# PSUM of a typed graph network: one standing tile for sums, weights and queries, two banks for node chains, and 806 gather slots in 49 blocks

## The chip, the cores and the metric

The kernel runs on one core of a Trainium2 chip. The time is the device time of one execution in microseconds (us), from the first instruction to the last and what lies around it. The engines are named as the profile names them: PE (matrix products) with its weight loads PEld, DVE (vector engine), ACT (scalar engine), POOL (GpSimd; here it issues the indirect DMAs, that is gathers and scatters of rows), SP (plain DMAs). SBUF is the working memory, PSUM the eight banks into which PE writes and which DVE and ACT read and write.

## The reference

A graph of 6,250 nodes (128 features, 16 node types) and 100,000 edges (32 edge types, sorted by target) goes through two layers of typed attention with 8 heads of 16 features, then a linear layer, a residual and a layer norm. The core of a layer:

```python
k = typed_linear(x, ntype, Wk).reshape(n, H, HS)      # the weight is chosen by the node's type
q = typed_linear(x, ntype, Wq).reshape(n, H, HS)
v = typed_linear(x, ntype, Wv).reshape(n, H, HS)
kT = jnp.einsum('nhd,htdo->nhto', k, Watt)            # for every node and every edge type
vT = jnp.einsum('nhd,htdo->nhto', v, Wmsg)
kw = kT[src, :, etype]
m = vT[src, :, etype]
a = jnp.einsum('ehd,ehd->eh', kw, q[dst]) * pri[:, etype].T / SQRT_D
att = edge_softmax(a, dst, n)                         # over the edges that end in one node
hag = jax.ops.segment_sum((m * att[:, :, None]).reshape(-1, H * HS), dst, num_segments=n)
h = jax.nn.silu(typed_linear(hag, ntype, Wa))
alpha = jax.nn.sigmoid(skip[ntype])[:, None]
h = h * alpha + x * (1.0 - alpha)
return layernorm(h) * g + b
```

All is float32.

## The kernel before

**Tables.** For each layer there is a table in DRAM with one row for each node and edge type: 128 numbers of kT and 128 of vT. An edge is one row of it, and so one row of a gather. Layer 0's table is made in the preparation. Layer 1's is made while layer 0's edges run: `table_block` (L342) multiplies the k and v of 128 nodes by the block-diagonal matrices `bdk` and `bdv` (PE, L354) into PSUM tiles "tb" of two banks, ACT copies each to the SBUF tile "st" (L362; in the last superblock DVE takes some, L360), and an indirect DMA from POOL's queue scatters "st" (L1761). A block of 128 nodes has two such scatters and eight "tb" tiles.

**Blocks and slots.** The preparation sorts the nodes by class (four classes of four node types) and by degree, and puts them into 49 blocks of 128. Each class has 11 blocks of its own, with 25, 21, 19, ... 11 slots (`OWN_SLOTS`, L47). A slot is one edge of each of the 128 nodes, so one gather of 128 rows. What a class's blocks don't hold goes to five mixed blocks of all 16 types (`MIXED_SLOTS`, L48). The first mixed block, `TOP`, has 42 slots, of which it gathers 26 and two more with shared rows, so 28. A layer has 819 gathers. If some block did not hold its nodes' degrees, the kernel would take a slow arm (`arm(False)`, L1916) that handles any graph.

**The edge loop** (`edges`, L1303, once for each layer) goes through the blocks in superblocks of up to four: each class's own, with a mixed superblock behind each of the first two classes. For every four slots (a chunk) it takes one of 12 "kv" tiles, issues four gathers (L1528), multiplies the k half by the block's query q (DVE, L1544) and sums over each head (L1550). When a block's chunks are through, the generator `finished` (L1365) does its softmax and its weighted sum while the next block's chunks run: mask, maximum, difference, exponential on ACT into w, sum "den", products of w and v, sums in "acc" (four slots wide), and the closing sum over these four. A "kv" tile comes free when its v half has been added.

**Node work.** When a superblock is finished, `nodes` (L1626) normalizes, transposes, applies Wa by type, mixes with the old rows, normalizes again, and in layer 0 makes the next k, v and q by type. A typed product is made of masks: for each type, DVE multiplies the node columns by (type == t) into one of four "xm" tiles (`masked`, L287), and PE adds the product with that type's weights to a PSUM tile "nb". Own superblocks have 4 types to go through, mixed ones 16. The queries of the next superblock are made the same way (`queries0`, L1281). All these steps are generators; `spread` and `tick` (L1312, L1316) deal them out among the chunks, so many steps for so many slots. `Held` (L257) keeps node work on DVE, ACT and PE behind the last instruction of the edge stream in program order; POOL's instructions run in program order; for the other engines the compiler's scheduler chooses the order.

**PSUM, eight banks.** In both layers: one bank for "nb" (pool `nps`, L1217), one for `hold`, three two-bank tiles "tb" (pool `tps`, L1220). In layer 0 q is read from SBUF, w lies in `hold`, "acc" in SBUF. In layer 1 each block takes a "tb" tile as `pair` (L1352): q and w in its second bank, "acc" in its first. `moved` (L1356) carries the shared rows of block `TOP` through PE.

Of the kernel before, what the change touches and what calls it, by code (L numbers as in the profile page):

```python
# [20 lines left out]
P = 128  # L21
# [25 lines left out]
OWN_SLOTS = (25, 21, 19, 18, 17, 16, 15, 15, 14, 12, 11)  # L47
MIXED_SLOTS = (42, 20, 16, 14, 9)  # L48
# [24 lines left out]
def kernel(  # L73
# [240 lines left out]
    def linear_of(pool, nps, types, ntb, hT, n, w):  # L314
# [3 lines left out]
        if len(types) > TC:  # L318
            h2 = pool.tile([P, SB * P], F32, name="h2", tag="hb")
            on.scalar.copy(h2[:, :n], hT[:, :n])  # L320
            yield
            hT = h2
# [880 lines left out]
    def arm(fast):  # L1203
# [13 lines left out]
        nps = ctx2.enter_context(tc.tile_pool(name="nps", bufs=1 if fast else 5, space=PSUM))  # L1217

        hold_ps = ctx2.enter_context(tc.tile_pool(name="hold", bufs=1, space=PSUM)) if fast else None
        tps = ctx2.enter_context(tc.tile_pool(name="tps", bufs=3, space=PSUM))  # L1220
# [82 lines left out]
        def edges(l):  # L1303
# [43 lines left out]
            def query(s, i):  # L1347


                if l == 0:  # L1350
                    return got[s][0][:, i, :], None
                pair = tps.tile([P, 2, SB * P], F32, name="tb")  # L1352
                nc.scalar.copy(pair[:, 1, :D], got[s][0][:, i, :])  # L1353
                return pair[:, 1, :D], pair

            def moved(pair, by, what, to):  # L1356


                n = what.shape[1]
                ps = pair[:, 1, D:D + n] if pair is not None else tps.tile(  # L1360
                    [P, 2, SB * P], F32, name="tb")[:, 0, :n]
                nc.tensor.matmul(ps, by, what, start=True, stop=True)
                nc.scalar.copy(to, ps)

            def finished(s, i, chunks, kvt, a, pair, sums, den):  # L1365
# [6 lines left out]
                if i0 + i == TOP:  # L1372
                    rest, chunks = kvt[-1], chunks[:-1]
                    moved(pair, node_of, rest[:, 3, :RK * REST * H],
# [13 lines left out]
                if rest is None:  # L1388
                    if l == 0:
                        held = hold_ps.tile([P, SB * P], F32, name="hold")  # L1390
                    w = (pair[:, 1, D:D + K * H] if l else held[:, :K * H]).rearrange(
                        "p (k h) -> p k h", h=H)
                on.scalar.activation(w, av, AF.Exp)
                if rest is not None:
                    moved(pair, rows_of, a[:, OWN:K, :].rearrange("p k h -> p (k h)"),
# [5 lines left out]
                if rest is None and l:  # L1401
                    acc = pair[:, 0].rearrange("p (k c) -> p k c", k=CH)
                else:
                    acc = ep.tile([P, CH, D], F32, name="acc", bufs=1)
# [23 lines left out]
                if rest is not None:  # L1428
# [14 lines left out]
                    moved(pair, node_of, rest[:, 2, D:], rest[:, 2, :D])  # L1443
# [7 lines left out]
                if i == k - 1:  # L1451
                    spread(work, nodes(l, *sbs[s], sums, den, *got[s][1:], lambda gen: table(s, gen)),
                           (42 if l else 33) + (0 if len(sbs[s][2]) == TC else 14 if l else 58),
# [39 lines left out]
            q, pair = query(0, 0)  # L1493
            for s, (i0, k, types) in enumerate(sbs):
                asked = None
                if s + 1 < len(sbs):
                    asked = queries(got, *sbs[s + 1])
                    spread(work, asked, 25 if mixed(s + 1) else 11 if l == 0 else 8, asking(s))
                sums = ep.tile([P, SB, D], F32, name="sums")
                den = ep.tile([P, SB, H], F32, name="den")  # L1500
                for i in range(k):
# [20 lines left out]
                    for j0, j1 in chunks:  # L1522
# [18 lines left out]
                        if rest:  # L1541
                            moved(pair, rows_of, got[s][0][:, i, :], kv[:, 2, :D])
# [24 lines left out]
                    before = finished(s, i, chunks, kvt, a, pair, sums, den)  # L1567
                    q, pair = then[0] if then else (None, None)
# [57 lines left out]
        def nodes(l, i0, k, types, sums, den, ntb, hr, table):  # L1626
# [46 lines left out]
            if not last:  # L1673
                if fast and i0 == sbs[0][0]:
                    scale_edge_weights()
                if fast and len(types) > TC:
# [6 lines left out]
                    for j in range(3):  # L1683
                        outs.append(nps.tile([P, SB * P], F32, name="nb"))
                        for t0 in range(0, TY, 2):
                            xms = list(masked(npl, types[t0:t0 + 2], ntb, h2, n))
                            yield
                            for t, xm in xms:
                                on.tensor.matmul(outs[j][:, :n], wkqv[:, j, t, :], xm[:, :n],
                                                 start=(t == 0), stop=(t == TY - 1))  # L1690
                            yield
                        if j < 2:
# [270 lines left out]
```

## Time and profile before

| | |
|---|---|
| median of 3 runs | 3025.17 us (3024.95 to 3028.88) |
| the profiled execution, its own time | 3024.62 us |
| its span, first to last instruction | 3022.8 us |
| POOL busy | 2032.2 us (67%) |
| DVE busy | 1891.1 us (63%) |
| PE busy | 1580.5 us (52%) |
| ACT busy | 978.7 us (32%) |
| gathers L1528 | 1638, mean 986 ns |

The span is that of one profiled execution, and 1.8 us of its own time lie around it. Busy is the time in which an engine's instructions ran; what an engine waited for is read from the waits, not from the shares. A gather's time in POOL's row is the time in which POOL makes its descriptors, not the transfer's.

### The profile page before, as it was taken

Reading aid. Unit: us, or ns where it says so; the run is one execution under the profiler, and the core shown is the slowest. Engines: PE = TensorE matmul, PEld = TensorE weight load, DVE = VectorE, ACT = ScalarE, POOL = GpSimd, SP = SyncE. Lnnn points to the kernel's source line nnn. Section 1 sums busy time; section 2 is a strip of 40 time slices with the busy share of each in tenths; the row PEclk is TensorE's granted clock in tenths of the full one; section 3 lists DMA queues with packets and bytes.
Section 4 is the critical chain, followed back from the end, with each engine's and each line's share of the span. In section 5 each row is a group of like instructions: output and inputs, shape, how many; then the busy total and the mean of one; then the engine's idle time right before and its main releaser. Section 6 shows DMA issues by size and latency. Waiting matters only on the chain.

```text
span 3022.8 us, 21562 instructions
## 1 busy us (share of the span) xinstructions
PE 1580.5 (52%) x5325; PEld 703.1 (23%) x5325; DVE 1891.1 (63%) x4383; ACT 978.7 (32%) x1635; POOL 2032.2 (67%) x2116
## 2 busy tenths in 40 slices
PE   5999978413667667777777884021122213221212
PEld 2445434201223322332223332010111001000001
DVE  7467655257657766777666653476576667666665
ACT  3887533200434234434444553011111111111111
POOL 3333665477777777777777762777677777777773
PEclk9999777556777777787777786555555556555555
DMA  7999999943677577867788897333334333333331
GB/s 217 416 418 418 394 392 397 371 107 100 234 275 260 197 248 282 297 225 254 271 303 296 330 354 278 105 110 111 92 103 118 111 111 109 112 109 106 106 100 45
DMA packets 163485, 671.37 MB, mean 222 GB/s; under 512 B 52012, under 2 KB 78926, under 8 KB 138302
## 3 DMA queue, kind: packets, MB, share of 16 engines
q0 software_dynamic: 113152, 635.19, 58.6%
q1 hardware_dynamic: 34218, 27.57, 3.3%
q10 hardware_dynamic: 15976, 7.10, 1.0%
q8 instruction: 46, 0.75, 0.1%
q14 instruction: 93, 0.76, 0.1%
HBM read 245.42 MB, written 425.02 MB: 222 GB/s over the span
## 4 chain that ended last, share of the span: by engine, by line
POOL 24%; issue 17%; DMA 16%; DVE 13%; PE 7%; ACT 3%; ACTq 0%; DVEq 0%; POOLq 0%
POOL kv L1528 21%; DMA kv<-tab,ell 14%; PE nb L267 6%; DVE kv L1544 2%; DVE xm L267 2%; PE tb L354 2%; DVE kv L267 2%; DMA tab<-st,row 2%; DVE a L1550 1%; DVE acc L267 1%; ACT L267 1%; POOL tab L1761 1%; DVE tb L267 1%; DVE hs L267 1%; POOL out_dram L1793 1%
## 5 line engine op out<-in xcount | busy, mean ns | idle before, releaser
L1528 POOL DMA_INDIRECT kv<-tab,ell x1638 | 1615.6, 986 | 542.6 <-issue 437.4
L362 ACT COPY st<-tb 128x512 f32<-128x512 f32 (+1 forms) x984 | 681.6, 777 | 535.4 <-PE tb L354 349.8
L1544 DVE TENSOR_TENSOR kv<-kv,tb 128x512 f32<-128x512 f32 (+3 forms) x223 | 142.7, 640 | 381.1 <-DMA kv<-tab,ell 367.4
L1544 DVE TENSOR_TENSOR kv<-kv,q 128x512 f32<-128x512 f32 (+3 forms) x223 | 142.9, 643 | 324.6 <-DMA kv<-tab,ell 316.1
L354 PE MATMUL tb<-bdv,vT 32*128 32x512 f32 x784 | 266.0, 781 | 45.0 <-ACT st L362 41.5
L1550 DVE TENSOR_REDUCE a<-kv 128x32 f32<-128x512 f32 (+3 forms) x446 | 280.8, 632 | 1.3
L354 PE MATMUL tb<-bdv,kvT 32*128 32x512 f32 x784 | 253.7, 790 | 22.9 <-ACT st L362 22.5
L354 PE MATMUL tb<-bdk,kvT 32*128 32x512 f32 x784 | 257.3, 776 | 7.9 <-ACT st L362 7.3
L267 PE MATMUL nb<-xm,wa 128*128 128x384 f32 (+2 forms) x336 | 178.0, 690 | 148.8 <-DVE xm L267 144.2
L267 PE MATMUL nb<-xm,wkqv 128*128 128x384 f32 (+2 forms) x504 | 218.6, 583 | 48.0 <-DVE xm L267 37.0
L1168 POOL DMA_INDIRECT tab<-st,rows x98 | 101.8, 1039 | 197.7 <-ACT st L362 169.4
L360 DVE COPY st<-tb 128x512 f32<-128x512 f32 (+1 forms) x192 | 128.7, 707 | 145.3 <-PE tb L354 74.7
L267 PE MATMUL nb<-by,all_rows 49*128 49x512 bf16 (+2 forms) x30 | 13.3, 442 | 381.6 <-DVE by L267 353.5
L354 PE MATMUL tb<-bdk,kT 32*128 32x512 f32 x784 | 210.6, 785 | 1.7 <-issue 1.6
L267 PE MATMUL nb<-ident,hag 128*128 128x128 f32 x98 | 24.6, 385 | 284.1 <-DVE hag L267 276.4
L1761 POOL DMA_INDIRECT tab<-st,row x98 | 106.1, 1083 | 80.4 <-DVE st L360 28.0
L267 PEld LDWEIGHTS nb<-xm,wkqv 128*128 128x128 f32 x504 | 106.4, 223 | 174.8 <-issue 88.6
L267 PEld LDWEIGHTS nb<-xm,wa 128*128 128x128 f32 x336 | 85.9, 272 | 240.6 <-issue 184.3
L267 DVE TENSOR_TENSOR tb<-kv,tb 128x512 f32<-128x512 f32 (+3 forms) x216 | 138.2, 640 | 0.2
L267 PE MATMUL nb<-xm,wq 128*128 128x384 f32 (+2 forms) x168 | 92.0, 708 | 87.2 <-DVE xm L267 87.1
L354 PEld LDWEIGHTS tb<-bdv,vT 32*128 32x128 f32 x784 | 98.8, 226 | 147.7 <-ACT st L362 118.9
L1353 ACT COPY tb<-hq 128x128 f32<-128x128 f32 x49 | 13.0, 267 | 369.4 <-DVE sums L267 268.8
(348 smaller groups left out, 2519.9 us busy)
## 6 DMA issues: line engine op xcount, KB each, us to landing
kv<-tab,ell POOLq DMA_INDIRECT x1638
hq<-hqx SPq DMA_DIRECT2D x7, 768.0 KB, 4.8
hqx<-hs SPq DMA_DIRECT2D x7, 512.0 KB, 3.5
hq<-hqx SPq DMA_DIRECT2D x5, 576.0 KB, 4.9
hqx<-xr SPq DMA_DIRECT2D x10, 256.0 KB, 19.2
hqx<-hs SPq DMA_DIRECT2D x5, 384.0 KB, 3.2
hr<-hqx SPq DMA_DIRECT2D x7, 256.0 KB, 5.6
tab<-st,rows POOLq DMA_INDIRECT x98
```

What stands on the lines that cost most here:

```text
L267: put = issue(*args, **kwargs)
L354: stream[nc.tensor] = nc.tensor.matmul(pt[:, b], yT[s, i * P:(i + 1) * P], bd[s, tt, :], start=True, stop=True)
L360: nc.vector.tensor_copy(to, pt)
L362: stream[nc.scalar] = nc.scalar.copy(to, pt)
L1168: put = nc.gpsimd.indirect_dma_start(out=tabs[0].rearrange("(n t) c -> n (t c)", t=16), out_offset=bass.IndirectOffsetOnAxis(ap=rows1[:, t ...
L1353: nc.scalar.copy(pair[:, 1, :D], got[s][0][:, i, :])
L1528: get = nc.gpsimd.indirect_dma_start(out=kv[:, j - j0, :], out_offset=None, in_=tabs[l][:], in_offset=bass.IndirectOffsetOnAxis(ap=ell[:, ...
L1544: stream[nc.vector] = nc.vector.tensor_tensor(kk, kk, of.unsqueeze(1).to_broadcast([P, c, D]), op=ALU.mult)
L1550: nc.vector.tensor_reduce(to, kk.rearrange("p k (h d) -> p k h d", h=H), axis=AX.X, op=ALU.add)
L1761: put = nc.gpsimd.indirect_dma_start(out=tabs[1].rearrange("(n t) c -> n (t c)", t=16), out_offset=bass.IndirectOffsetOnAxis(ap=row2[:, tg ...
L1793: put = nc.gpsimd.indirect_dma_start(out=out, out_offset=bass.IndirectOffsetOnAxis(ap=node[:, b:b + 1], axis=0), in_=o[:, i, :], in_offset ...
```

## The change

Three things change, in both layers unless it says otherwise.

1. *Slots.* Each class has ten blocks of its own (21 to 11 slots), and nine blocks are mixed, in three superblocks behind the first three classes. The number of blocks stays 49; the slots that are gathered go from 819 to 806.
2. *PSUM.* "nb" gets two banks instead of one, "tb" two tiles instead of three. The other two banks are one tile `held` that stands for the whole run: bank 0 for "acc", bank 1 for w (first half) and for the queries, which take turns in the last two quarters. ACT copies each block's q there, in layer 0 too. `moved` always takes a "tb" tile.
3. *Mixed node work.* `linear_of` no longer copies a transposed "nb" tile to SBUF before the masks, which read PSUM instead. For k, v and q of a mixed superblock, k and v share one round of masks (32 masks instead of 48), which read the SBUF copy as before. The step counts given to `spread` follow.

```diff
-OWN_SLOTS = (25, 21, 19, 18, 17, 16, 15, 15, 14, 12, 11)
-MIXED_SLOTS = (42, 20, 16, 14, 9)
+OWN_SLOTS = (21, 19, 18, 17, 16, 15, 14, 13, 12, 11)
+MIXED_SLOTS = (42, 25, 24, 23, 22, 20, 16, 15, 9)
...
         types = list(types)
-        if len(types) > TC:
-            h2 = pool.tile([P, SB * P], F32, name="h2", tag="hb")
-            on.scalar.copy(h2[:, :n], hT[:, :n])
-            yield
-            hT = h2
         some, ps = 2 if len(types) > TC else TC, None
...
-        nps = ctx2.enter_context(tc.tile_pool(name="nps", bufs=1 if fast else 5, space=PSUM))
-
-        hold_ps = ctx2.enter_context(tc.tile_pool(name="hold", bufs=1, space=PSUM)) if fast else None
-        tps = ctx2.enter_context(tc.tile_pool(name="tps", bufs=3, space=PSUM))
+        nps = ctx2.enter_context(tc.tile_pool(name="nps", bufs=2 if fast else 5, space=PSUM))
+
+        turn, held = [0], None
+        if fast:
+            hold_ps = ctx2.enter_context(tc.tile_pool(name="hold", bufs=1, space=PSUM))
+            held = hold_ps.tile([P, 2, SB * P], F32, name="held")
+            assert max(OWN, *KB[:TOP], *KB[TOP + 1:]) * H <= 2 * D
+        tps = ctx2.enter_context(tc.tile_pool(name="tps", bufs=2 if fast else 3, space=PSUM))
...
             def query(s, i):
-                if l == 0:
-                    return got[s][0][:, i, :], None
-                pair = tps.tile([P, 2, SB * P], F32, name="tb")
-                nc.scalar.copy(pair[:, 1, :D], got[s][0][:, i, :])
-                return pair[:, 1, :D], pair
-
-            def moved(pair, by, what, to):
+                at = (2 + turn[0] % 2) * D
+                turn[0] += 1
+                nc.scalar.copy(held[:, 1, at:at + D], got[s][0][:, i, :])
+                return held[:, 1, at:at + D]
+
+            def moved(by, what, to):
                 n = what.shape[1]
-                ps = pair[:, 1, D:D + n] if pair is not None else tps.tile(
-                    [P, 2, SB * P], F32, name="tb")[:, 0, :n]
+                ps = tps.tile([P, 2, SB * P], F32, name="tb")[:, 0, :n]
                 nc.tensor.matmul(ps, by, what, start=True, stop=True)
                 nc.scalar.copy(to, ps)
...
                 w = av
                 if rest is None:
-                    if l == 0:
-                        held = hold_ps.tile([P, SB * P], F32, name="hold")
-                    w = (pair[:, 1, D:D + K * H] if l else held[:, :K * H]).rearrange(
-                        "p (k h) -> p k h", h=H)
+                    w = held[:, 1, :K * H].rearrange("p (k h) -> p k h", h=H)
                 on.scalar.activation(w, av, AF.Exp)
...
-                if rest is None and l:
-                    acc = pair[:, 0].rearrange("p (k c) -> p k c", k=CH)
-                else:
-                    acc = ep.tile([P, CH, D], F32, name="acc", bufs=1)
+                acc = held[:, 0].rearrange("p (k c) -> p k c", k=CH)
...
-                           (42 if l else 33) + (0 if len(sbs[s][2]) == TC else 14 if l else 58),
+                           (42 if l else 33) + (0 if len(sbs[s][2]) == TC else 13 if l else 41),
...
-                    spread(work, asked, 25 if mixed(s + 1) else 11 if l == 0 else 8, asking(s))
+                    spread(work, asked, 24 if mixed(s + 1) else 11 if l == 0 else 8, asking(s))
...
                     outs = []
-                    for j in range(3):
-                        outs.append(nps.tile([P, SB * P], F32, name="nb"))
+                    for js in ((0, 1), (2,)):
+                        outs += [nps.tile([P, SB * P], F32, name="nb") for _ in js]
                         for t0 in range(0, TY, 2):
                             xms = list(masked(npl, types[t0:t0 + 2], ntb, h2, n))
                             yield
                             for t, xm in xms:
-                                on.tensor.matmul(outs[j][:, :n], wkqv[:, j, t, :], xm[:, :n],
-                                                 start=(t == 0), stop=(t == TY - 1))
+                                for j in js:
+                                    on.tensor.matmul(outs[j][:, :n], wkqv[:, j, t, :], xm[:, :n],
+                                                     start=(t == 0), stop=(t == TY - 1))
                             yield
-                        if j < 2:
+                        for j in js[:2 - js[0]]:
                             to = npl.tile([P, SB * P], F32, name=f"kvT{j}", bufs=2)
                             on.scalar.copy(to[:, :n], outs[j][:, :n])
                             outs[j] = to
```

With the new lists a class's own superblocks are (21, 19, 18), (17, 16, 15), (14, 13, 12, 11), in the last class (13, 12, 11), (16, 15, 14), (18, 17), (21, 19); the mixed ones are (42, 25, 24), (23, 22, 20), (16, 15, 9). Before, they were (18, 17, 16, 15), (15, 14, 12, 11), (25, 21, 19), in the last class (15, 14, 12, 11), (17, 16, 15), (19, 18), (25, 21); the mixed ones (42, 20) and (16, 14, 9).

## Rows read from the trace of the kernel before

**Rows 1.** Stages: us from:to, length, busy us (instructions) of each engine.

```profile
core 0: us, PE busy (x) PEld busy (x) DVE busy (x) ACT busy (x) POOL busy (x), PEclk, DMA share, GB/s
600.00:1778.00 1178.00, 807.39 (x2492) 328.32 (x2492) 780.16 (x1707) 453.99 (x617) 905.02 (x884) 0.74 0.71 248
1778.00:1875.00 97.00, 66.21 (x233) 28.94 (x233) 44.62 (x95) 44.70 (x58) 28.21 (x29) 0.73 0.83 329
1875.00:2977.00 1102.00, 210.75 (x463) 106.29 (x463) 694.10 (x1693) 146.53 (x302) 827.55 (x864) 0.54 0.37 108
```

**Rows 2.** Timeline of POOL, layer 1: start us, us, instruction, idle before.

```profile
2303.78 0.94 POOL L1528 DMA_INDIRECT kv<-tab,ell  x1 [0.30 <-issue]
```

**Rows 3.** POOL's waits, 600 to 1778 us: us in total, times, longest us.

```profile
POOL kv L1528 <- issue: 209.9, 689, 0.3
...
POOL tab L1761 <- ACT st L362: 5.1, 10, 2.1
```

**Rows 4.** POOL's groups, 600 to 1875 us: busy us, mean ns, idle before.

```profile
L1528 POOL DMA_INDIRECT kv<-tab,ell x815 | 828.4, 1016 | 261.7 <-issue 214.2 <-DMA tab<-st,row 13.6 <-DMA kv<-tab,ell 11.2
L1761 POOL DMA_INDIRECT tab<-st,row x98 | 106.1, 1083 | 80.4 <-DVE st L360 28.0 <-issue 25.8 <-ACT st L362 22.4
```

**Rows 5.** POOL's groups, 1875 us to the end.

```profile
L1528 POOL DMA_INDIRECT kv<-tab,ell x819 | 782.1, 955 | 272.4 <-issue 222.1 <-DVE t L267 12.8 <-DMA tab<-st,row 12.2
```

**Rows 6.** Timeline of DVE and POOL at two places of layer 0.

```profile
1055.07 0.69 DVE L1544 TENSOR_TENSOR kv<-kv,q 128x512 f32<-128x512 f32 x1 [1.25 <-DMA kv<-tab,ell]
1055.19 1.39 POOL L1528 DMA_INDIRECT kv<-tab,ell  x1 [0.30 <-issue]
...
1101.40 0.68 DVE L267 TENSOR_TENSOR acc<-kv,acc 128x512 f32<-128x512 f32 x1
1101.62 1.27 POOL L1528 DMA_INDIRECT kv<-tab,ell  x1 [0.30 <-issue]
```

**Rows 7.** DVE's groups by shape, 600 to 1875 us.

```profile
L1544 DVE TENSOR_TENSOR kv<-kv,q 128x512 f32<-128x512 f32 x184 | 126.8, 689 | 298.4 <-DMA kv<-tab,ell 290.0 <-ACT q L267 7.6 <-issue 0.6
...
L267 DVE TENSOR_TENSOR acc<-kv,acc 128x512 f32<-128x512 f32 x135 | 92.2, 683 | 0.0
...
L267 DVE TENSOR_REDUCE sums<-acc 128x128 f32<-128x512 f32 x49 | 51.0, 1041 | 0.1
L267 DVE SCALAR_TENSOR_TENSOR xm<-ntb,h 128x384 f32<-128x384 bf16 x80 | 41.1, 551 | 8.6 <-PE nb L267 4.0 <-ACT h L267 3.8
...
L267 DVE SCALAR_TENSOR_TENSOR xm<-ntb,h 128x256 f32<-128x256 bf16 x80 | 30.1, 414 | 5.6 <-PE nb L267 5.4 <-ACT h L267 0.2
```

**Rows 8.** DVE's groups by shape, 1875 us to the end.

```profile
L1544 DVE TENSOR_TENSOR kv<-kv,tb 128x512 f32<-128x512 f32 x184 | 126.2, 686 | 360.4 <-DMA kv<-tab,ell 346.7 <-issue 13.4
...
L267 DVE TENSOR_REDUCE sums<-tb 128x128 f32<-128x512 f32 x48 | 32.5, 678 | 0.0
```

**Rows 9.** DVE's waits, 600 to 1875 us.

```profile
DVE kv L1544 <- DMA kv<-tab,ell: 316.1, 125, 7.0
...
DVE den L267 <- ACT hold L267: 21.3, 7, 9.5
```

**Rows 10.** ACT's groups by shape, 600 to 1875 us.

```profile
L362 ACT COPY st<-tb 128x1024 f32<-128x1024 f32 x384 | 372.9, 1020 | 329.5 <-PE tb L354 276.8 <-DMA tab<-st,row 43.4 <-issue 7.2
```

**Rows 11.** ACT's groups by shape, 1875 us to the end: the copy of q.

```profile
L1353 ACT COPY tb<-hq 128x128 f32<-128x128 f32 x49 | 13.0, 267 | 369.4 <-DVE sums L267 268.8 <-DVE rd L267 59.5 <-issue 24.5
```

**Rows 12.** PE's groups by shape, 600 to 1875 us: masked matmuls of three-block superblocks.

```profile
L267 PE MATMUL nb<-xm,wkqv 128*128 128x384 f32 x192 | 81.0, 569 | 15.6 <-DVE xm L267 13.6 <-ACT kvT L267 1.5
```

**Rows 13.** Timeline of PE in the turn: the two matmuls of one "tb" tile.

```profile
1844.38 1.12 PE L354 MATMUL tb<-bdk,kvT 32*128 32x512 f32 x2
```

**Rows 14.** POOL's waits, 1778 to 1875 us.

```profile
POOL tab L1761 <- DVE st L360: 28.0, 2, 26.5
```

**Rows 15.** Line 354 alone, 600 to 1875 us: PE busy, PEld busy.

```profile
600.00:1875.00 1275.00, 429.90 (x1568) 126.61 (x1568) 0.74 0.72 254
```

**Rows 16.** POOL's waits, 1875 us to the end.

```profile
POOL kv L1528 <- DVE t L267: 12.8, 6, 11.3
```

More of the change, by code (lines that the diff above doesn't have):

```diff
@@ L1347, in query, with finished @@
             def query(s, i):
-                if l == 0:
-                    return got[s][0][:, i, :], None
-                pair = tps.tile([P, 2, SB * P], F32, name="tb")
-                nc.scalar.copy(pair[:, 1, :D], got[s][0][:, i, :])
-                return pair[:, 1, :D], pair
-            def moved(pair, by, what, to):
+                at = (2 + turn[0] % 2) * D
[3 more added lines that the diff above has]
+            def moved(by, what, to):
                 n = what.shape[1]
-                ps = pair[:, 1, D:D + n] if pair is not None else tps.tile(
-                    [P, 2, SB * P], F32, name="tb")[:, 0, :n]
+                ps = tps.tile([P, 2, SB * P], F32, name="tb")[:, 0, :n]
                 nc.tensor.matmul(ps, by, what, start=True, stop=True)
                 nc.scalar.copy(to, ps)
-            def finished(s, i, chunks, kvt, a, pair, sums, den):
+            def finished(s, i, chunks, kvt, a, sums, den):
                 i0, k, _ = sbs[s]
@@ L1373, in finished @@
                     rest, chunks = kvt[-1], chunks[:-1]
-                    moved(pair, node_of, rest[:, 3, :RK * REST * H],
+                    moved(node_of, rest[:, 3, :RK * REST * H],
                           a[:, OWN:K, :].rearrange("p k h -> p (k h)"))
@@ L1388, in finished @@
                 if rest is None:
[L1389 to L1392 removed]
+                    w = held[:, 1, :K * H].rearrange("p (k h) -> p k h", h=H)
                 on.scalar.activation(w, av, AF.Exp)
                 if rest is not None:
[L1395 removed]
+                    moved(rows_of, a[:, OWN:K, :].rearrange("p k h -> p (k h)"),
                           rest[:, 3, :RK * REST * H])
@@ L1442, in finished @@
                                             op=ALU.add)
-                    moved(pair, node_of, rest[:, 2, D:], rest[:, 2, :D])
+                    moved(node_of, rest[:, 2, D:], rest[:, 2, :D])
                     yield
@@ L1492, in edges @@
             before = iter(())
-            q, pair = query(0, 0)
+            q = query(0, 0)
             for s, (i0, k, types) in enumerate(sbs):
@@ L1541, in edges @@
                         if rest:
-                            moved(pair, rows_of, got[s][0][:, i, :], kv[:, 2, :D])
+                            moved(rows_of, got[s][0][:, i, :], kv[:, 2, :D])
                         of = kv[:, 2, :D] if rest else q
@@ L1566, in edges @@
                         step(end=True)
-                    before = finished(s, i, chunks, kvt, a, pair, sums, den)
-                    q, pair = then[0] if then else (None, None)
+                    before = finished(s, i, chunks, kvt, a, sums, den)
+                    q = then[0] if then else None
             for _ in before:
```

## The prediction

> **What bounds the kernel now.** I read the table of stages first [rows 1]. It splits the span: preparation to about 600 us, layer 0's edges to 1778, the turn to layer 1 (97 us), layer 1's edges (1102 us), and a tail of 46 us. In both edge stages POOL is the fullest engine. The busy share hides that it is in truth full: after each gather POOL sits idle for 0.30 us that wait on nothing [rows 2], and in layer 0 its waits are 209.9 us of that kind, in 689 pieces of at most 0.3 us, and next to nothing else [rows 3]. So an instruction costs POOL its own time plus 0.30 us: layer 0's body 905.0 + 884 x 0.30 = 1170 of 1178 us, layer 1's 827.6 + 864 x 0.30 = 1087 of 1102 [rows 1]. POOL's cadence sets both.
>
> The gathers differ, though: 1.016 us each in layer 0 [rows 4], 0.955 in layer 1 [rows 5]. Why is to be seen in the timeline [rows 6]. A gather that starts at 1055.19, while the DVE product kv*q (two operands in SBUF; start 1055.07, 0.69 us) runs, takes 1.39 us instead of 0.95. Another, beside the sum acc+kv (SBUF and SBUF, 1101.40 to 1102.08), takes 1.27. Both gathers end about 0.82 us after that DVE instruction's end: they stood still until then. In layer 1 the queries and sums lie in PSUM ("tb").
>
> **The change part by part.**
>
> *Fewer slots.* In each layer the gathers fall from 819 to 806 (4 x 156, and 182 in the mixed blocks, since block TOP fetches 28 for its 42). 13 gathers at 0.95 + 0.30 = 1.25 us are 16.3 us in each layer, both on the path: -32.5 us. The slots still hold the graph: I counted the degrees of the reference's inputs by class. 1130 nodes overflow into the mixed blocks' 1152 places, and no block's largest degree is over its slots. So the fast arm runs.
>
> *Standing tile for sums, weights and queries.* In layer 0, q and acc move from SBUF to PSUM; layer 1 had them there. DVE's product takes the same time (689 [rows 7] against 686 ns [rows 8]). The closing sum takes 678 ns from PSUM [rows 8] instead of 1041 from SBUF [rows 7]: 48 x 0.36 = 17 us off DVE, which waited 316 us for gathers [rows 9], so worth nothing by itself. POOL gains: 806 gathers at layer 1's mean would save 806 x 61 ns = 49 us. The DVE instructions with two SBUF operands that can hold a gather up are, in full widths, kv*q 126.8, acc 92.2 and the masks xm from SBUF 41.1 + 30.1: 290 us [rows 7]. The first two go. Of the masks, the rounds for wq and wa of mixed superblocks now read PSUM; 3 x 32 = 96 from SBUF stay, x 0.551 = 53 us. That is 18% of the 290, and 18% of the 49 are 9 us. I take -40 us, with ends 0 (the length has another cause) and -49.
>
> On this the Trainium skill (SBUF — State Buffer, Who interferes with whom) says that a VectorE instruction with two SBUF inputs contends with a GpSimd instruction that reads SBUF, but it also infers that tensor_tensor does not hold up descriptor generation, because that needs the write interface. The gathers of [rows 6] go against that inference; by it the 40 us would not be had and the sum would be 3002 us, which is rival 2.
>
> *Waits that the standing tile adds.* Each of layer 0's 49 blocks gets an ACT copy of q, 267 ns as in layer 1 [rows 11]: 13 us on an ACT that is busy 454 of 1178 us [rows 1]. Queries and softmax weights of all blocks now share a bank. If accesses are ordered by bank, as I assume, the copy of the next q waits for the product kv*q before it, and the product after it waits for the copy; the exponential likewise stands between two products. Queued behind the copy on ACT are the table copies, for which PE's next table matmuls wait, then the node matmuls behind those; behind the product on DVE is everything, and POOL waits when kv tiles stay taken. The nearest row is layer 0's "den" waiting for the exponential: 21.3 us in 7 waits [rows 9]. The upper end is that for both, 43 us; it lies in 316 us of DVE's idle time, and gathers may run ahead by 12 kv tiles (48 gathers). I take 0.
>
> The skill has a rule that speaks against this part (PSUM — Partial Sum Buffer, PSUM bank collisions raise a hardware error): guard PSUM by bank and quadrant, not by address. Without it (order by address) the copy waits for nothing and the sum stands; by it, if half of the 43 us came through to POOL, the sum would be 2984 us, inside the range. No row of before shows which, since there each block of layer 1 had its own tile.
>
> *Two "tb" tiles instead of three.* A tile takes PE about 1.12 us to fill [rows 13] and ACT 1.02 us to empty [rows 10]. With two, PE fills one while ACT empties the other; with some 0.3 us of handovers the pair turns in 2.4 us, 1.2 a tile; ACT alone would need 1.02. In the body a block's 8 tiles have some 20 us: nothing. In the turn, where POOL waits 28.0 us for table copies [rows 14], the last superblock's 16 tiles stand on the path: 16 x 0.2 = 3 us, upper end 8 (ACT and DVE empty in parallel there, so both openings show).
>
> *Two "nb" tiles instead of one.* A chain's matmuls start at the first mask instead of after the last, and k, v and q no longer wait for the copy before: about 1 us a chain (of 4 masks of some 0.35 us, three wait no more), on the path only in the turn (-1, at most -4) and the tail (-1). Turn together: +2, ends -4 and +8. The tail's last block has 19 slots instead of 21, another 0.7 us: tail -2.
>
> *Nine mixed blocks instead of five.* They make three superblocks with all 16 types instead of two. In layer 0 each costs 64 masks (80 before). That matters where this work meets few gathers. After the third one (16, 15, 9) comes (13, 12, 11): 36 slots x 1.25 + 8 table writes x 1.38 [rows 4] = 56 us of POOL. DVE must do 48 masks x 0.551 = 26 us, 36 slots x 0.68 (four instructions of 0.68 us per four slots [rows 7]) = 24.5, and about 10 of small steps: 61. PE has 64 + 4 matmuls at 0.42 (81.0 us for 192 [rows 12]) = 29, and the tables of four blocks at 429.9/49 = 8.8 [rows 15]: 64. Both are 5 to 8 us over. The densest window of before, behind (16, 14, 9), (64 masks, 66 slots, 6 writes) is by the same count DVE 92 to POOL's 91, and POOL waited for nothing. I charge +10; ends 0 (the kv tiles bridge it) and 30 (twice both excesses, late table writes with it). The windows after the other two have 58 slots and some 5 us to spare.
>
> In layer 1 a mixed superblock costs 16 masks; with one more that is 9 us in a DVE busy 694 of 1102 us [rows 1]: nothing. The wait of 11 to 13 us behind block TOP [rows 16] stays: its kv tiles come free no sooner.
>
> **Sum.** The profiled execution took 3024.62 us (span 3022.8, 1.8 around it), half a microsecond under the median of 3025.17. 3024.6 - 32.5 - 40 + 2 - 2 + 10 = 2962 us.
>
> **Rivals.**
> 1. *Layer 0 becomes bound by DVE and PE.* Faster gathers only reach table writes or kv tiles that are not ready. For: PE is busy 807 of 1178 us [rows 1], and its masked matmuls grow by a fifth (per block 20 rounds of 128 columns for an own one, 80 for a mixed one: 1280 to 1520). Against: in that stage POOL waited 5.1 us for ACT [rows 3], DVE 316 us for gathers. If layer 0 keeps a quarter of its 56 us: 3024.6 - 16 - 14 - 2 = 2992.
> 2. *The long gathers have another cause:* the 40 us stay, 3002 us. Against: the gathers' ends follow DVE's ends.
> 3. *Slower: two tb tiles become the clock of layer 0.* If ACT and PE alternate, 1.12 + 0.3 - 1.02 = 0.4 us per tile is open; 392 tiles (384 and 8) make 157 us, paid by POOL at the table writes: 3024.6 - 74 + 157 = 3108. It decides from the point where 47% of these openings reach POOL. For: filling takes longer than emptying. Against: ACT's table copies fill 372.9 us of the stage [rows 10].
> 4. *The slots don't hold the graph* and the slow arm runs: many times as long. The count above speaks against it.
>
> **Chances and range.** Forecast 0.67 (its own range 2943 to 2982), rival 1 0.20, rival 2 0.05, rival 3 0.07, rival 4 0.01. Low end: all 49 of the gathers, a turn 4 shorter, no stall: 3024.6 - 32.5 - 49 - 2 - 4 = 2937, taken as 2940. High end: 30 of the gathers, stall 30, turn +8, tail as it was: 3000; rivals 3 and 4 and most of 2 stay outside. Within 0.2% (6 us) is what a measurement of this kernel can't tell from no change. Faster: forecast, rivals 1 and 2, less 0.03 for a rival 1 that eats all of it: 0.89; same 0.04; slower 0.07 (rival 4 and most of 3).
>
> **What would show it.** 806 gathers in each layer at the same 0.30 us; layer 0's mean gather near 0.967 us, long ones only beside masks from SBUF; layer 1's stage 16 us shorter; "sums" at 0.68 us in layer 0; any POOL wait of layer 0 in the window behind (16, 15, 9). It is wrong if POOL waits for "st" or for kv tiles all over layer 0, if gathers stay at 1.016, or if DVE waits for ACT's q copies by more than 43 us and POOL with it.

## The result, and the profile after

The changed kernel takes 3034.38 us (median of 9 runs, 3025.92 to 3038.66), the kernel before beside it 3026.26 us (9 runs, 3021.51 to 3032.2). The ratio is 1.0025, 95% interval 1.0013 to 1.0037: 8 us slower, where 2962 us, 2.1% faster, were forecast. The profiled execution took 3037.24 us, 12.6 more than that of before; the accounts below are made against these two.

The table of stages, cut at the last gather of layer 0 and the first of layer 1:

```profile
core 0: us, PE busy (x) PEld busy (x) DVE busy (x) ACT busy (x) POOL busy (x), PEclk, DMA share, GB/s
600.00:1811.00 1211.00, 922.59 (x2640) 371.42 (x2641) 806.63 (x1769) 472.77 (x678) 856.03 (x888) 0.72 0.70 242
1811.00:1913.00 102.00, 78.84 (x247) 33.47 (x247) 32.27 (x63) 45.67 (x60) 12.96 (x14) 0.65 0.73 294
1913.00:2988.00 1075.00, 215.45 (x503) 111.53 (x503) 716.64 (x1719) 153.44 (x308) 815.17 (x851) 0.55 0.37 109
```

[rows 1] cuts the kernel before at 1778 us, 23 us ahead of its last gather of layer 0. Up to that gather the kernel before has:

```profile
600.00:1801.00 1201.00, 828.70 (x2550) 338.31 (x2550) 794.08 (x1741) 468.42 (x634) 922.55 (x902) 0.74 0.71 250
```

So layer 0's body is longer although POOL has less to do in it: it is busy 856 of 1211 us, where it was busy 923 of 1201. POOL's groups in the changed kernel's body (the gather is now line 1519, the table write line 1753), and its waits:

```profile
L1519 POOL DMA_INDIRECT kv<-tab,ell x802 | 768.4, 958 | 251.8 <-issue 204.1 <-DVE held L267 11.7 <-DMA kv<-tab,ell 10.4
L1753 POOL DMA_INDIRECT tab<-st,row x86 | 88.6, 1030 | 103.5 <-ACT st L357 78.1 <-issue 16.6 <-ACT ntb L267 3.5
```

```profile
POOL kv L1519 <- issue: 204.1, 670, 0.3
POOL tab L1753 <- ACT st L357: 78.1, 20, 16.2
...
POOL kv L1519 <- DVE held L267: 11.7, 17, 6.8
```

The gathers did become short: 958 ns on average against 1016 [rows 4]. But the cadence, one instruction after the other with 0.3 us between them, is broken. Where POOL waited 5.1 us for ACT's table copies [rows 3], it now waits 78.1 us, in pieces of up to 16.2 us. The timeline of DVE and POOL shows what became of the gathers of [rows 6]; these masks, the sum and the product now have a PSUM operand, and gathers that start beside them take 0.94 us:

```profile
702.96 1.94 DVE L267 SCALAR_TENSOR_TENSOR xm<-ntb,nb 128x384 f32<-128x384 bf16 x4
703.04 0.94 POOL L1519 DMA_INDIRECT kv<-tab,ell  x1 [0.30 <-issue]
...
705.74 0.70 DVE L267 TENSOR_TENSOR held<-kv,held 128x512 f32<-128x512 f32 x1
706.78 0.94 POOL L1519 DMA_INDIRECT kv<-tab,ell  x1 [0.30 <-issue]
707.12 0.69 DVE L1535 TENSOR_TENSOR kv<-kv,held 128x512 f32<-128x512 f32 x1 [0.69 <-DMA kv<-tab,ell]
```

Another stretch, in the second superblock behind the second mixed one, shows what the table writes wait for (timeline of PE, ACT and POOL):

```profile
1329.60 5.32 PE L267 MATMUL nb<-xm,wkqv 128*128 128x384 f32 x16
1334.85 1.14 PE L349 MATMUL tb<-bdv,kvT 32*128 32x512 f32 x8
1335.92 5.43 PE L267 MATMUL nb<-xm,wkqv 128*128 128x384 f32 x16
1336.05 1.93 ACT L357 COPY st<-tb 128x1024 f32<-128x1024 f32 x2 [7.81 <-PE tb L349]
1338.26 1.01 POOL L1753 DMA_INDIRECT tab<-st,row  x1 [11.72 <-ACT st L357]
1339.57 1.35 POOL L1519 DMA_INDIRECT kv<-tab,ell  x1 [0.30 <-issue]
...
1342.35 7.32 PE L267 MATMUL nb<-xm,wkqv 128*128 128x384 f32 x20
...
1349.60 1.14 PE L349 MATMUL tb<-bdv,kvT 32*128 32x512 f32 x8
...
1350.80 1.93 ACT L357 COPY st<-tb 128x1024 f32<-128x1024 f32 x2 [2.50 <-PE tb L349]
1353.00 1.35 POOL L1753 DMA_INDIRECT tab<-st,row  x1 [8.25 <-ACT st L357]
```

POOL stands 11.72 us at one write and 8.25 at the next. It waits for ACT, ACT had waited 7.81 us for PE, and PE was never idle: between two pairs of "tb" tiles (1.14 us of table matmuls) it runs 5 to 7 us of the mixed superblock's masked matmuls.

The loss sits where such stretches are. Between 600 and 1811 us POOL's idle time beyond 0.31 us per instruction adds up to 84.7 us (before: 3.6); 68.5 us of it lie in these three stretches, one behind each mixed superblock:

```profile
core 0: us, PE busy (x) PEld busy (x) DVE busy (x) ACT busy (x) POOL busy (x), PEclk, DMA share, GB/s
1004.00:1067.00 63.00, 51.69 (x196) 22.11 (x196) 45.49 (x98) 32.42 (x46) 41.69 (x43) 0.91 0.70 251
1278.00:1366.00 88.00, 81.59 (x259) 35.30 (x258) 63.34 (x137) 34.07 (x46) 52.39 (x54) 0.83 0.66 238
1541.00:1660.00 119.00, 110.00 (x333) 47.67 (x332) 79.58 (x180) 48.13 (x69) 64.57 (x67) 0.83 0.64 234
```

PE is busy 243 of these 270 us (90%), DVE 188. In the middle of each PE makes k, v and q of the mixed superblock, and there it has no gap at all, 120.7 of 121 us:

```profile
core 0: us, PE busy (x), PEclk, DMA share, GB/s
988.00:1029.00 41.00, 40.84 (x139) 0.96 0.56 207
1321.00:1363.00 42.00, 41.86 (x140) 0.94 0.49 178
1615.00:1653.00 38.00, 38.00 (x126) 0.94 0.39 138
```

By the gathers' count these bursts lie not in the superblock that follows the mixed one (908 to 992, 1238 to 1322, 1542 to 1602 us), but nearly whole in the one after it (992 to 1078, 1322 to 1414, 1602 to 1695). POOL lost 1.0, 0.1 and 7.9 us in the first kind and 14.7, 21.9 and 26.4 us in the second. PE is the bound there.

### The profile page after: what moved, and what is told of

The parts are those of the page before. It is cut to its first block, busy times and chain, and to the rows that moved or that the text cites. A ratio compares the mean times of both kernels' runs of the same rounds, so it can differ in the third digit from the quotient of the medians.

```text
span 3035.3 us, 22161 instructions
## 1 busy us (share of the span) xinstructions
PE 1712.3 (56%) x5523; PEld 752.7 (25%) x5523; DVE 1923.8 (63%) x4429; ACT 1005.2 (33%) x1702; POOL 1953.3 (64%) x2090
## 4 chain that ended last, share of the span: by engine, by line
POOL 19%; issue 16%; DVE 16%; PE 14%; DMA 12%; ACT 4%; DVEq 0%; POOLq 0%; ACTq 0%
POOL kv L1519 17%; DMA kv<-tab,ell 11%; PE nb L267 8%; PE tb L349 5%; DVE kv L1535 3%; DVE kv L267 3%; DVE held L267 3%; DVE a L1541 2%; ACT st L357 2%; DVE xm L267 2%; DVE hs L267 1%; ACT L267 1%; DMA tab<-st,row 1%; POOL tab L1753 1%; POOL out_dram L1785 1%
## 5 line engine op out<-in xcount | busy, mean ns | idle before, releaser
L1519 POOL DMA_INDIRECT kv<-tab,ell x1612 | 1543.7, 958 | 527.3 <-issue 416.1
L1535 DVE TENSOR_TENSOR kv<-kv,held 128x512 f32<-128x512 f32 (+3 forms) x440 | 281.0, 640 | 548.6 <-DMA kv<-tab,ell 466.6
L267 DVE TENSOR_TENSOR held<-kv,held 128x512 f32<-128x512 f32 (+3 forms) x438 | 283.1, 646 | 8.8
L349 PE MATMUL tb<-bdv,vT 32*128 32x512 f32 x784 | 259.0, 781 | 46.6 <-ACT st L357 42.8
L267 PE MATMUL nb<-xm,wkqv 128*128 128x384 f32 (+2 forms) x600 | 245.8, 568 | 10.3 <-DVE xm L267 10.2
L267 PE MATMUL nb<-xm,wa 128*128 128x384 f32 (+2 forms) x400 | 201.6, 666 | 85.0 <-DVE xm L267 80.6
L267 PE MATMUL nb<-by,all_rows 49*128 49x384 bf16 (+2 forms) x32 | 14.7, 458 | 385.6 <-DVE by L267 359.8
L267 DVE TENSOR_TENSOR kv<-kv,held 128x512 f32<-128x512 f32 (+3 forms) x330 | 204.7, 621 | 2.0
L267 DVE SCALAR_TENSOR_TENSOR xm<-ntb,nb 128x384 f32<-128x384 bf16 (+2 forms) x352 | 179.4, 555 | 41.5 <-PE nb L267 39.8
L267 PEld LDWEIGHTS nb<-xm,wkqv 128*128 128x128 f32 x600 | 127.4, 220 | 138.4 <-DVE xm L267 40.7
L267 PEld LDWEIGHTS nb<-xm,wa 128*128 128x128 f32 x400 | 99.4, 261 | 186.6 <-issue 84.7
L267 PE MATMUL nb<-xm,wq 128*128 128x384 f32 (+2 forms) x200 | 116.0, 736 | 51.0 <-DVE xm L267 51.0
L267 PE MATMUL nb<-ident,hs 128*128 128x128 f32 x98 | 33.8, 465 | 178.5 <-DVE hs L267 178.5
## 6 DMA issues: line engine op xcount, KB each, us to landing
hqx<-xr SPq DMA_DIRECT2D x10, 256.0 KB, 14.7
```

Of the source, the lines that this page charges most:

```text
L267: put = issue(*args, **kwargs)
L349: stream[nc.tensor] = nc.tensor.matmul(pt[:, b], yT[s, i * P:(i + 1) * P], bd[s, tt, :], start=True, stop=True)
L1519: get = nc.gpsimd.indirect_dma_start(out=kv[:, j - j0, :], out_offset=None, in_=tabs[l][:], in_offset=bass.IndirectOffsetOnAxis(ap=ell[:, ...
L1535: stream[nc.vector] = nc.vector.tensor_tensor(kk, kk, of.unsqueeze(1).to_broadcast([P, c, D]), op=ALU.mult)
```

## The experiments

Each kernel's profiled execution is cut at four starts of gathers: the first and last of layer 0, the first and last of layer 1. In the table "lost" is POOL's idle time beyond 0.31 us per instruction between the first two, and "long" the time by which its instructions there exceed 0.95 us, summed; "writes" are the table writes after layer 0's last gather. All in us, worked out from the traces; the ratio is to the kernel before, run beside each. Masks or matmuls that a kernel leaves out are missing from its results, so the kernels with four types, without masks and without matmuls only show where the time goes.

| kernel | layer 0 | lost | long | turn | writes | layer 1 | tail | median | ratio, 95% |
|---|---|---|---|---|---|---|---|---|---|
| before | 1209.3 | 3.6 | 70.4 | 73.6 | 9 | 1100.9 | 47.4 | 3026.26 | 1 |
| changed | 1217.3 | 84.7 | 17.7 | 101.5 | 12 | 1074.8 | 47.5 | 3034.38 | 1.0025, 1.0013 to 1.0037 |
| lists alone | 1251.9 | 66.0 | 70.6 | 92.2 | 12 | 1088.8 | 50.4 | 3079.40 | 1.0178, 1.0156 to 1.0200 |
| PSUM alone | 1166.2 | 15.1 | 16.4 | 87.0 | 9 | 1090.3 | 42.9 | 2978.74 | 0.9849, 0.9827 to 0.9870 |
| two "tb" alone | 1221.3 | 11.0 | 75.1 | 82.1 | 9 | 1104.1 | 47.1 | 3048.64 | 1.0075, 1.0049 to 1.0101 |
| changed, four types | 1154.6 | 24.0 | 14.7 | 98.1 | 11 | 1074.4 | 46.8 | 2973.65 | 0.9824, 0.9803 to 0.9846 |
| PSUM alone, four types | 1156.4 | 5.4 | 15.0 | 83.0 | 8 | 1090.1 | 41.8 | 2966.41 | 0.9809, 0.9791 to 0.9826 |
| changed, longer window | 1215.7 | 81.9 | 19.0 | 99.3 | 12 | 1075.1 | 46.5 | 3026.27 | 1.0002, 0.9992 to 1.0012 |
| changed, no masks | 1197.3 | 69.3 | 13.2 | 103.6 | 12 | 1074.4 | 47.0 | 3018.03 | 0.9985, 0.9975 to 0.9996 |
| changed, no matmuls | 1162.0 | 25.9 | 21.2 | 104.2 | 12 | 1074.7 | 46.6 | 2982.28 | 0.9852, 0.9832 to 0.9872 |

**First attempt, on another chip.** Four kernels were run together: before with the new lists; the changed kernel with the old lists; before with two "tb" tiles; and the changed kernel with three "tb" tiles, for which "nb" goes back to one bank and the sums back to SBUF.

> The kernel before with the new lists of slots alone (819 to 806 gathers, nine mixed blocks); PSUM as before. Theory A (the nine mixed blocks' 16-type work fills PE and DVE, tables come late, POOL waits at the table writes behind each mixed superblock): no gain of the gathers' length, 16 us from layer 1, layer 0 longer by some 60 to 80: 3070 to 3090 us. Theory B (two tb tiles slow the tables down): no new wait here, the 32 us of 26 gathers are had: 2993 to 3000. Theory C (the shared bank puts ACT's copies of q and the exponentials between DVE's products): as B, 2993 to 3000.

> The changed kernel with the old lists of slots (819 gathers, five mixed blocks); PSUM as changed. A: layer 0 keeps the shorter gathers (53 us less held up) and few waits: 2970 to 2990 us. B: tables late all over layer 0 and in the turn, 3050 to 3080. C: DVE waits for ACT's copies as much as in the changed kernel (64 us) and tables are late as there, 3040 to 3060.

> The kernel before with two tb tiles instead of three and nothing else (two banks lie idle; layer 1's blocks take turns in two tiles as well). A: 3026 to 3032. B: POOL waits for st all over layer 0 and the turn is some 15 us longer: 3070 to 3110. C: 3026 to 3032.

> The changed kernel with three tb tiles, for which the sums go back to SBUF in layer 0 and 1, nb to one bank and the mixed masks to rounds for one product each; new lists, and q and w still in one standing bank. A: POOL waits behind the mixed superblocks as in the changed kernel, plus some 17 us of gathers held up by the sums in SBUF and more masks: 3045 to 3070. B: the waits are gone: 2980 to 2995. C: DVE still waits for the copies, 3040 to 3060.

On that chip the kernel before itself took 3404.8 us (7 runs, 3392.3 to 3419.96). The ratios were 1.0229 (1.0163 to 1.0295), 1.0220 (1.0172 to 1.0268), 1.0139 (1.0075 to 1.0204) and 1.0217 (1.0166 to 1.0267). Everything is slower, and in both layers POOL lost 164 to 327 us. The timeline of the run with two "tb" tiles shows a kind of wait that neither trace of the first chip has:

```profile
2710.27 0.18 DVE L267 BATCH_NORM_AGGREGATE mv<-bn 128x2 f32<-128x6 f32 x1 [1.22 <-DVE mv L267]
...
2715.17 0.17 DVE L267 TENSOR_SCALAR v<-mv 128x4 f32<-128x4 f32 x1 [4.13 <-remote]
2715.17 0.30 ACT L267 ACTIVATE rs<-mv,eps 128x4 f32<-128x4 f32 x1 [5.73 <-remote]
```

Both instructions need only mv, made by 2710.45, and both start at 2715.17. With such waits between the engines POOL is not full anywhere, so these four runs cannot separate the theories. The first three kernels were run again on another chip, where the kernel before takes 3026 us; the runs below are from there and from a third chip, where it takes 3025. One thing carried over: "long" was 73.7 and 82.8 us with queries and sums in SBUF, 16.8 with both in PSUM, 54.8 in the fourth kernel, with the queries there alone and all masks read from SBUF.

**The two halves, and two "tb" tiles.** One half of the change each, by the lists or by everything else:

```diff
 # lists alone: before, with
+OWN_SLOTS = (21, 19, 18, 17, 16, 15, 14, 13, 12, 11)
+MIXED_SLOTS = (42, 25, 24, 23, 22, 20, 16, 15, 9)
 # PSUM alone: the changed kernel, with
+OWN_SLOTS = (25, 21, 19, 18, 17, 16, 15, 15, 14, 12, 11)
+MIXED_SLOTS = (42, 20, 16, 14, 9)
 # two "tb" alone: before, with
+        tps = ctx2.enter_context(tc.tile_pool(name="tps", bufs=2 if fast else 3, space=PSUM))
```

> The kernel before with the new lists of slots alone (806 slots, nine mixed blocks in three superblocks), all PSUM tiles as before; the edit of the first experiment on another chip, whose cross-engine waits were lengthened there. Theory A (the mixed blocks' work of sixteen types makes the tables late, in the window behind each mixed superblock and in the turn): the 32 fewer gathers are more than eaten, ratio 1.005 to 1.02 on a chip where before takes some 3025 us, with GpSimd waiting some 80 us or more for ScalarE's st copies in layer 0. Theory B (two table tiles in place of three make the tables late): the lists alone gain their slots, ratio 0.985 to 0.992, and GpSimd's wait for st stays near the 5 us of before. Theory C (queries, weights and sums in one standing tile put ScalarE's copies and VectorE's products behind one another): as B.

> The changed kernel with the old lists of slots (819 slots, five mixed blocks): all the moves in PSUM, none in the lists. Theory A: the gathers' hold-ups of some 53 us in layer 0 fall away and the tables keep up, ratio 0.978 to 0.987. Theory B: the tables are late with the old lists too, ratio 1.00 to 1.01, GpSimd waiting 80 us or more for st in layer 0. Theory C: the gathers' gain is given back at VectorE, which waits for ScalarE's copies into the standing tile; ratio 0.995 to 1.005 with the loss in both layers.

> The kernel before with two table tiles in place of three and nothing else (two banks stand empty). Theory A: ratio 0.999 to 1.005. Theory B: ratio 1.01 to 1.03 with GpSimd waiting for st. Theory C: ratio 0.999 to 1.003.

The halves add up: +53 us for the lists, -47 for the PSUM part, +6 together, and the whole measured +8. Both ratios lie where theory A put them; POOL's wait for table copies with the lists alone is 56.7 us, less than A's 80. That wait in layer 0's body, lists alone, PSUM alone and two "tb" tiles alone (gathers' waits of the PSUM kernel beside it):

```profile
POOL tab L1761 <- ACT st L362: 56.7, 16, 12.1
```

```profile
POOL tab L1753 <- ACT st L357: 15.5, 18, 6.7
POOL kv L1519 <- DVE held L267: 4.9, 10, 2.2
```

```profile
POOL tab L1761 <- ACT st L362: 13.7, 13, 3.9
```

Theory B has a smaller share of its own: with two tiles alone the kernel is 23 us slower, 12 of them in layer 0's body (7.4 as "lost", 4.7 as "long") and 8.5 in the turn. That is between what A and B expected. Theory C falls: it expected a ratio of 0.995 or more for the PSUM kernel with a loss in both layers, and the ratio is 0.9849 and layer 1 is 10.6 us shorter. These three runs say that the lists cost; the next tell which part of them.

**Four types in the mixed blocks.** The twelve other types' masks and matmuls are left out:

```diff
-            mixed = [(NC * CB + i0, k, range(TY)) for i0, k in superblocks(MB)]
+            mixed = [(NC * CB + i0, k, range(TC)) for i0, k in superblocks(MB)]
```

> The changed kernel whose mixed blocks are computed with the four node types of the first class alone, where the reference has sixteen: twelve of sixteen masked products of each of their linear maps are left out in both layers, and the mixed superblocks count as ordinary ones in the interleaving. Gathers, tables and PSUM tiles are those of the changed kernel. Theory A: with that work gone the tables are in time and the gathers run through, ratio 0.955 to 0.972, GpSimd's wait for st in layer 0 back under 15 us outside the turn. Theory B: the tables stay late, ratio 0.995 or more. Theory C: ratio 0.985 to 0.995.

> The changed PSUM tiles with the old lists (five mixed blocks), the mixed blocks computed with the four types of the first class alone, where the reference has sixteen. With nine mixed blocks the same omission gave 61 us. Theory A with a threshold (a mixed superblock's work costs nothing until the window behind it is full): five blocks were hidden, so only 5 to 20 us are gained on the same kernel with sixteen types, ratio 0.978 to 0.983. Rival, a price in proportion to the mixed blocks: 5/9 of 61 us, some 34 us, ratio 0.972 to 0.975.

With nine mixed blocks the twelve types cost 61 us (ratio 1.0025 to 0.9824), with five 12 us (0.9849 to 0.9809; by the two intervals 4 to 21). The 61 us are less than theory A's number, whose lowest gain was 92 us: the turn is still 24.5 us longer than before, and "lost" is 24.0 us, where it was 3.6. That the two "tb" tiles are behind the latter is not shown. The ratio for five blocks lies in the range given for the threshold, outside that of a price in proportion. In the nine-block kernel 62.7 us of it come from layer 0's body and 3.4 from the turn: the turn's length is not the types' doing.

**Which engine.** In the changed kernel the masks beyond the first two types are left out and the first two used for all, or the matmuls beyond the fourth type are left out and the masks made:

```diff
 # no masks (linear_of; the same in nodes for k, v and q)
-            xms = list(masked(pool, types[t0:t0 + some], ntb, hT, n))
+            if t0 == 0:
+                made = list(masked(pool, types[:some], ntb, hT, n))
+            xms = [(t, xm) for t, (_, xm) in zip(types[t0:t0 + some], made)]
 # no matmuls (linear_of; the same in nodes)
+                if t - types[0] < TC:
                     on.tensor.matmul(ps[:, :n], w[:, t, :], xm[:, :n],
-                                 start=(t == types[0]), stop=(t == types[-1]))
+                                     start=(t == types[0]), stop=(t == types[0] + TC - 1))
```

> The changed kernel in which the mixed blocks' masked products (xm) are made for the first two types alone and used for all sixteen, so that 14 of 16 masks of each of their linear maps are left out (some 93 us of VectorE in layer 0) and every matmul and every step of the interleaving stays. Theory A1 (TensorE is what the tables wait for): within 15 us of the changed kernel, ratio 0.998 to 1.004. Theory A2 (VectorE's masks hold the tables and products up): 40 to 60 us less than the changed kernel, ratio 0.982 to 0.990. Theory A3 (the number of steps per slot in the interleaving, whatever they contain): as A1.

> The changed kernel in which the mixed blocks' masks are all made and 12 of 16 matmuls of each of their linear maps are left out (some 102 us of TensorE in layer 0); masks and steps stay. Theory A1: 40 to 60 us less than the changed kernel, ratio 0.982 to 0.990. Theory A2: within 15 us of it, ratio 0.998 to 1.004. Theory A3: within 15 us too, as in the run without masks.

Without the matmuls 52 of the 61 us are gone (ratio 1.0025 to 0.9852), though every mask is made; without the masks 12 us (to 0.9985), although DVE has 80 us less to do (726.2 against 806.6 us busy in the body). POOL's wait for table copies, no masks and then no matmuls, and PE's masked matmuls in the latter:

```profile
POOL tab L1757 <- ACT st L359: 60.6, 16, 15.3
```

```profile
POOL tab L1754 <- ACT st L358: 22.7, 17, 7.4
```

```profile
L267 PE MATMUL nb<-xm,wkqv 128*128 128x384 f32 x264 | 121.2, 625 | 10.4 <-DVE xm L267 10.4
```

Theory A1, TensorE, holds. Theory A3 (the number of steps, which both kernels keep) falls with the run without matmuls. One rival within A1 stays untested: the run takes away PE's work and, with it, the bursts that table matmuls wait behind. No run keeps the work and changes its order, so how much of the 52 us a better order would give back is not known.

**A longer window behind the third mixed superblock.** (16, 15, 14) now stands before (13, 12, 11):

```diff
-                    cut = [(i0 + SB, k) for i0, k in
-                           reversed(superblocks_of_slots(OWN_SLOTS[SB:]))]
+                    cut = [(i0 + SB, k) for i0, k in superblocks_of_slots(OWN_SLOTS[SB:])]
```

> The changed kernel with one change of order: behind the third mixed superblock comes (16, 15, 14), 45 slots, and then (13, 12, 11), 36 slots, where it was the other way. If the short window behind the third mixed superblock is what costs (the prediction's reading), the loss of some 32 us there falls by 10 to 20 us, ratio 0.995 to 1.000. Rival: the work only runs on into the next window, which is now the short one, and the sum stays, ratio 1.001 to 1.005.

The ratio is 1.0002 (0.9992 to 1.0012), between the two. In the profiled executions "lost" fell only from 84.7 to 81.9 us. POOL's losses behind the first two mixed superblocks stay: 36.7 us between 1000 and 1450 us in the changed kernel, 40.3 here; behind the third 34.3 us (1550 to 1700) became 30.1 (1550 to 1750). So the reading that the third window carries it is not borne out: all three do. The longer window also stands in the wrong place: the third burst of PE still runs from 1616 to 1660 us, which is now in the superblock of 36 slots (1618 to 1690), where 18.3 of the 30.1 us are lost.

## Why the prediction was wrong

It failed in the step on nine mixed blocks, charged at +10 us and at most 30: the lists alone made POOL lose 62 us more in layer 0 (3.6 to 66.0), and the twelve further types cost 61 us of the changed kernel. Two things in that step are wrong.

The first is the price of a matmul: "PE has 64 + 4 matmuls at 0.42 (81.0 us for 192 [rows 12]) = 29". The 192 are records, not matmuls. Each of these fp32 products stands in the trace as two. For k, v and q at 384 columns the program issues 16 x 3 for a mixed superblock of three blocks and 4 x 3 for one of its own class. Before that is 48 + 4 x 12 = 96, and the row has 192; after it is 3 x 48 + 8 x 12 = 240, and the row has 480:

```profile
L267 PE MATMUL nb<-xm,wkqv 128*128 128x384 f32 x480 | 188.7, 551 | 9.3 <-DVE xm L267 9.2
```

So the price is 0.84 us, not 0.42, and the step's own sum for the window behind (16, 15, 9) becomes 57 + 35 = 92 us of PE to POOL's 56: 36 over, not 8. For the windows of 58 slots the same count gives 57 + 26 = 83 us of PE to 58 x 1.25 + 6 x 1.38 = 81 of POOL, before transposes: about full, not "some 5 us to spare". Before, behind (16, 14, 9), it is 83 to POOL's 91. The Trainium skill (FP8 and Floating Point Precision, TensorE Precision Notes) says that true FP32 takes four passes through the array. By it, at one column a tick, 384 columns are 1536 ticks, an estimate of 0.64 us at 2.4 GHz and 1.28 at 1.2; the row above has 188.7 / 240 = 0.79 us in a stage with a mean granted clock of 0.72, and 16 records at 1335.92, in a burst with a mean of 0.94, take 5.43 us, 0.68 for each matmul, so the trace agrees.

The second is the place: the step puts all the matmuls of a mixed superblock into the superblock behind it. In the trace those for k, v and q, 48 of the 64, come nearly whole in the one after that. The corrected price alone would give the first two windows 2 us of loss each; what they lost behind them was 14.7 and 21.9. In the superblocks in which the bursts lie PE is busy 74.5, 81.5 and 85.3 us, and by the prediction's prices POOL's work is 48 x 1.25 + 7 x 1.38 = 70 us in the first two and 66 in the third. So PE is over in all three, and that the corrected 36 comes near the 34.3 us lost behind the third mixed superblock is in part luck. (The step's DVE sum for the window of before, 92, comes to 90 by its own terms; nothing hangs on it.)

The other terms:

- *Fewer slots, -32.5:* right. Layer 0's body has 16 POOL instructions less (13 gathers, and 3 writes that moved to the turn), layer 1 13 gathers less.
- *The gathers' length, -40 (0 to -49):* right mechanism, undersized and past its own end: "long" fell by 52.7 us with the change and 54.0 with the PSUM part alone; the table writes became shorter too (1030 against 1083 ns [rows 4]), which the term left out. These runs go against rival 2 and against the inference of the Trainium skill that the prediction names beside it (SBUF — State Buffer, Who interferes with whom).
- *The standing tile's waits, 0 (43 on DVE):* bigger on DVE than the upper end, and still nearly free for POOL. DVE's waits in layer 0's body:

```profile
DVE kv L1535 <- DMA kv<-tab,ell: 175.4, 68, 7.1
DVE kv L1535 <- ACT held L1351: 64.1, 29, 6.2
...
DVE den L267 <- ACT held L267: 37.0, 16, 8.8
```

  101 us where 43 was the bound. DVE's wait for gathers went from 316 us [rows 9] to 175; with the old lists, where this arrangement is the same, POOL lost 15.1 us in all. The order that the prediction assumed is not what the trace shows: where ACT's copies of q waited, it was once for the product kv*q (0.8 us), and else for the closing sum of the block before, whose operand lies in the other bank of the tile:

```profile
ACT held L1351 <- DVE sums L267: 84.1, 19, 12.5
```

- *Two "tb" tiles, 0 in the body and +3 in the turn:* too small; alone they cost 12.0 us and 8.5 us. The body's "some 20 us for a block's 8 tiles" takes PE as free whenever a tile is; it runs other matmuls in between. The count of records misled here too: the 1568 of [rows 15] stand for 49 blocks of 8 tiles with two matmuls each, so the two of [rows 13] are one matmul, half a tile, and above, at 1334.85, eight records, so two tiles, take 1.14 us. Rival 3's "filling takes longer than emptying" does not hold there.
- *The turn, +2 net (-4 to +8):* +27.9. The PSUM part alone gives +13.4 and the lists alone +18.6, with 12 table writes after the last gather instead of 9. No step of the prediction had the lists act there. The last two superblocks now have 35 and 40 slots of gathers over their tables' work instead of 37 and 46, which would leave more writes behind; that is argued, and no run here tried it.
- *Layer 1, 0 beyond the slots; the wait behind block TOP stays:* wrong, in the kernel's favour. That wait of 11 us is gone in both kernels with the standing tile, and there with the lists alone and the two "tb" tiles alone. So layer 1 is 26.1 us shorter, not 16.3.
- *The tail, -2:* 0.1 longer.

Added up on the profiled executions: layer 0 from its first gather to its last -20 (16 x 1.25) - 52.7 + 81.1 = +8, turn +27.9, layer 1 -26.1, preparation +2.6, tail +0.1: +12.5 us of span.

Rival 1 was nearest: layer 0 became bound by PE. It left layer 0 a quarter of its gain, on an average of PE's work over the whole stage; the work comes in three bursts, and the loss (81.1 us) was larger than the gain (73). Rival 3's mechanism is real at 20 us, not 157. What stays open is why the lists lengthen the turn, what of the two "tb" tiles' cost is left once PE has room, and what another order of PE's work would save.

The PSUM part with the old lists beats both kernels: 2978.74 us, 47 us less than the kernel before.

## What to carry to other kernels

Count an engine's work in the program's instructions and check that the trace's count is the same before dividing a busy time by it: a factor of two in one row turned a window that had room into one that was full. Put that count window by window, since an engine that is 76% busy over a stage was 90% busy in the three windows that set the time; and look in the trace of before in which window the work falls, since here it came one superblock later than assumed. A change made of parts with opposite signs is best split in the first experiment; here the halves were -47 and +53 us.

## What the runs showed of the hardware

An fp32 product stands in the trace as two records of the same shape (a transpose as one: 98 for the 49 blocks of two layers); 384 columns took 0.79 us for the two at a mean granted clock of 0.72. A gather that starts while a VectorE instruction with two SBUF operands runs can be held until that has ended, tensor_tensor and scalar_tensor_tensor alike: in layer 0 of the kernel before, 33 of the 56 gathers that started while a product kv*q of 128x512 ran took over 1.15 us, and 27 of these ended 0.80 to 0.85 us after it; in the changed kernel, with q in PSUM, none of 39 did. With product and sum moved to PSUM, 53 of 70 us of such delay in layer 0 went. And one chip ran the kernel before in 3404.8 us where the others took 3025 to 3026: the preparation was as long there (592.7 to 594.3 us to the first gather in the four kernels, 591.7 in the kernel before on the first chip); the time was lost in the stages where the engines wait for one another in short steps. Why that chip does so is open.
